# Clipped differences from stage one through DRAM, row statistics in the feed-forward, and cross attention in the order logits, values, transposes

## The chip, the cores and the metric

The kernel runs on one core of a Trainium2 chip. Its time is the device time of one execution in microseconds (us); lower is better. Before the change the median of three runs is 951.55 us (951.16 to 952.6). Five engines work side by side, each through its own list of instructions in program order: TensorE (PE; its weight loads are listed apart as PEld), VectorE (DVE), ScalarE (ACT), GpSimd (POOL) and SyncE (SP), which here issues all transfers. A "shape" such as 32*128 behind a matmul is the part of the TensorE array that it uses.

## What is computed

One decoder layer in float32, on 16 sequences of 256 tokens of width 256 (4096 rows). `n()` is a row norm without parameters; cut to what matters:

```python
# stage one: "attention" of 4 heads of 64 against 256 fixed keys and values
xn = n(x) * ln_g + ln_b
h  = n(2 * x + values(square(relu(scores(xn)))))
# cross attention: 16 heads of 16, keys and values from ctx of the same sequence
D    = clip(frac[:, None, :] - frac[:, :, None], -0.2, 0.2)
bias = alpha_pos * max(D, 0) + alpha_neg * min(D, 0)      # per head
attn = gamma * (Q K^T) / 4 + delta * bias
h    = n(h + softmax(attn) V Wo^T + bo)
# feed-forward: the arg-max gate of 8 chooses a rank-4 addition inside the relu
out  = n(h + relu(h Wi^T + bi + lora[top1]) Wo2^T + bo2)
```

The clipped differences, `min(D, 0)` and `max(D, 0)`, depend on `frac` alone. They are the same for all 16 heads of a sequence and need neither stage one nor the context.

## The kernel before

All work stands under a manual schedule: each engine executes its instructions in the order in which the Python code emits them, and only semaphores hold an engine back. So the order of the calls in the main loops is the order on every engine's list.

**Stage one** (about 12 to 258 us) takes 8 blocks of 512 tokens, each in 8 steps `m` of two pieces. A step's scores (L306), the relu on ACT (L314) and the square on DVE (L316) feed the next step's values matmuls (L326). What else belongs to a step (statistics, norms, turns of neighbouring blocks) is put into the list `steps[m]`, which is worked off after the step's matmuls. The result stays in SBUF as `hid`.

**Cross attention** (about 258 to 668 us) runs over 16 batches (the sequences) of 4 groups of 4 heads, in one loop over iterations `n`. The names of its parts, with their lines:

- `logits` (L583): 8 matmuls of shape 32*128 that add to four PSUM banks, `banks[0..3]`, in which `positive` (ACT, L574) has already put `alpha_pos * max(D, 0)`, one instruction for each of the four heads. A bank's `positive` for the next group can start only when its maxima are done.
- `negative` (L562 on POOL for three heads, L567 on ACT for the fourth) makes `alpha_neg * min(D, 0)`.
- `maxima` (DVE, L597): 8 instructions, each adds `neg` to half a bank, writes `t` to SBUF and gives the row maximum. `subtract` (L612) takes the maximum away, two heads on POOL and two on DVE.
- `turned(g)`: 4 transposes (PE, L621) of one head, and the exponential (ACT, L626) that brings them to `pT`.
- `attend` (PE, L635): 16 weight loads of shape 128*32; the weights are the probabilities' counterpart `va`, values with a column block of ones, so that the sums of the softmax come with the products. `keep` copies the two halves of a batch's result to `raw` (ACT, L648), and after the second half `gather` sends it through SP: sums (L493) and values `v` in 8 transfers (L501).
- `invert` (DVE L509; SP: rows L511, invs in 8 transfers L517) and `divide` (DVE L524) give the normalised heads; `project` (PE L531, DVE L540) adds the output projection to `hid`; `stats` makes the row statistics of the sum (L194 and L195, two rows of 128 tokens).
- For the next batch: `load` (context `cT` L392 and fractions `frow` L394), the hidden-state turn `turned` of the batch (4 transposes L403, ACT copy L410), `queries` (PE L416, ACT L426), `keys` (PE L436, DVE L446, then 8 transfers `kM` on SP, L452), `vals` (PE L458, DVE copy L466) and the two clips `below` and `above` (DVE L473).

PSUM has four logits banks, one for `attend`, and a ring of three banks from `tile_b()` that all else shares in turn: whoever gets a bank waits until the third allocation before it has been read.

An iteration emits, before the change: logits(n); transposes 2 and 3 of group n-1; negative(n+1); maxima(n); positive 0 and 1; subtract(n); positive 2 and 3; the large piece of this iteration; attend(n-1); transposes 0 and 1 of n; keep(n-1); further small work. The `pieces` function says which: a batch's first group has the hidden-state turn as small piece and `project` as large piece, the second `queries`, the third `keys`, the fourth `vals`; `invert` and `below` are at the second group, `above` at the third, `divide` at the fourth, `stats` at the first.

**The feed-forward** (about 668 to 948 us) takes 8 blocks of 512 tokens: `norm` (from the statistics in `mv2`), turn, gates, `inner`, `lora`, `outer`, and the final norm and store, each block's parts between those of its neighbours.

## Time and profile before

| | |
|---|---|
| median of 3 runs | 951.55 us (951.16 to 952.6) |
| the profiled execution | 950.16 us |
| its span, first to last instruction | 948.3 us (1.86 us lie around it) |
| granted TensorE clock | 0.99 |
| busy PE, DVE, ACT, POOL | 910.5, 692.3, 582.5, 427.4 us |
| period of a group of the cross attention | 5.90 to 5.92 us, at a batch's first group 6.38 us |
| a batch | 24.10 us undisturbed, 24.29 us on average over batches 2 to 13 |

How to read the profile: it is one execution, its times in us from the span's start. A line of the timeline gives start, length, engine, source line, operation, output<-inputs, shape and, after x, how many instructions in a row it stands for; in brackets is the idle time before it and who ended it. A line of the window view gives a stretch, its length, then busy time and number of instructions for PE, PEld, DVE, ACT and POOL, and last the granted clock, the share of the DMA engines and GB/s. "SPq" lines are issues of transfers on SP's queue. The chain of waits follows the work that ended last back to its start and shares out the span over engines.

### The profile page before, as it was taken

The numbers are of one execution on the slowest core, as the hardware profiler recorded it, in microseconds if no ns is written. First come the engines' busy times: TensorE is split into PE (matmuls) and PEld (weight loads), VectorE is DVE, ScalarE is ACT, GpSimd is POOL, SyncE is SP. The second block draws the span as 40 slices with busy tenths as digits, with TensorE's granted clock in tenths as the row PEclk, the third lists the DMA queues.
The fourth block names the chain that finished last, engine by engine and source line by source line (L and its number), as shares of the span: only waits on it lengthen the run. The fifth ranks groups of instructions, "written<-read, shape, count | busy, mean of one in ns | idle before, by whom it ended". The sixth has DMA issues, their size and how long they took to land.

```text
span 948.3 us, 19070 instructions
## 1 busy us (share of the span) xinstructions
PE 910.5 (96%) x6910; PEld 547.2 (58%) x6910; DVE 692.3 (73%) x1893; ACT 582.5 (61%) x970; POOL 427.4 (45%) x352
## 2 busy tenths in 40 slices
PE   5999999999988999999999999998789999999997
PEld 2333333333356677777777777775336566665656
DVE  4787879888777999999999999998523344343324
ACT  4757787677779899999999999997101010101010
POOL 1002321223467898999988889995101101110100
PEclk9999999999989999999999999999899999999999
DMA  5300000100101122222222222111100000000001
GB/s 156 116 23 23 8 17 23 40 2 2 28 1 40 46 51 52 54 53 53 53 53 53 53 51 54 47 43 25 24 1 0 23 23 2 21 23 23 1 22 45
DMA packets 42461, 33.85 MB, mean 36 GB/s; under 512 B 14720, under 2 KB 39808, under 8 KB 42368
## 3 DMA queue, kind: packets, MB, share of 16 engines
q1 hardware_dynamic: 41648, 31.85, 12.7%
q8 instruction: 55, 0.90, 0.4%
q10 hardware_dynamic: 720, 0.79, 0.4%
q14 instruction: 38, 0.31, 0.1%
HBM read 19.50 MB, written 4.46 MB: 25 GB/s over the span
## 4 chain that ended last, share of the span: by engine, by line
PE 88%; DVE 4%; ACT 3%; POOL 3%; issue 1%; DMA 1%; SPq 0%; POOLq 0%; ACTq 0%; DVEq 0%
PE ps_b L621 13%; PE ps_l L774 12%; PE ps_a L306 12%; PE ps_v L326 11%; PE ps_v L804 10%; PE ps_l L583 7%; PE ps_v L635 5%; PE ps_b L531 3%; PE ps_b L436 3%; POOL t L612 2%; PE ps_b L416 2%; PE ps_b L458 2%; PE ps_l L786 2%; DVE t L597 2%; PE ps_b L804 1%
## 5 line engine op out<-in xcount | busy, mean ns | idle before, releaser
L562 POOL TENSOR_SCALAR neg<-dneg,aneg,delta 128x512 f32<-128x512 f32 x192 | 228.0, 1198 | 0.0
L597 DVE CUSTOM_DVE_ANT_0 t<-ps_l,neg 128x256 f32<-128x256 f32 x512 | 181.5, 419 | 13.1 <-PE ps_l L583 6.6
L316 DVE TENSOR_TENSOR pr<-r 128x1024 f32<-128x1024 f32 x128 | 155.2, 1253 | 42.3 <-ACT r L314 42.1
L314 ACT ACTIVATE r<-ps_a 128x1024 f32<-128x1024 f32 x128 | 126.5, 1023 | 60.8 <-PE ps_a L306 36.4
L574 ACT ACTIVATE ps_l<-dpos,apos_d 128x512 f32<-128x512 f32 x256 | 162.8, 689 | 1.7 <-DVE mx L597 1.6
L626 ACT ACTIVATE pT<-ps_b 128x512 f32<-128x512 f32 x256 | 137.4, 594 | 32.8 <-PE ps_b L621 32.7
L621 PE MATMUL ps_b<-ident,t 128*128 128x128 f32 x1024 | 142.0, 282 | 11.7 <-POOL t L612 10.1
L621 PEld LDWEIGHTS ps_b<-ident,t 128*128 128x128 f32 x1024 | 110.9, 142 | 61.5 <-POOL t L612 33.5
L612 POOL TENSOR_TENSOR t<-t,mx 128x1024 f32<-128x1024 f32 x64 | 121.1, 1893 | 52.8 <-DVE mx L597 49.1
L306 PE MATMUL ps_a<-xnT,kT 64*64 64x512 f32 x1024 | 123.5, 597 | 0.2
L326 PE MATMUL ps_v<-pr,vv 64*64 64x512 f32 x1024 | 122.7, 592 | 0.0
L774 PE MATMUL ps_l<-xt,wi 128*128 128x512 f32 x256 | 114.4, 600 | 0.0
L704 POOL TENSOR_TENSOR x<-x,wofb 128x256 f32<-128x256 f32 x32 | 22.2, 730 | 202.7 <-PE ps_b L698 202.7
L793 ACT ACTIVATE hT<-ps_l,wib 128x512 f32<-128x512 f32 x32 | 20.3, 684 | 151.9 <-PE ps_l L786 137.4
L612 DVE TENSOR_TENSOR t<-t,mx 128x1024 f32<-128x1024 f32 x64 | 111.8, 1747 | 2.2
L804 PE MATMUL ps_v<-wof,hT 128*128 128x256 f32 x448 | 101.4, 382 | 0.0
L804 PEld LDWEIGHTS ps_v<-wof,hT 128*128 128x128 f32 x448 | 83.5, 190 | 18.9 <-issue 8.4
L338 POOL TENSOR_TENSOR xt<-xt,half 128x512 f32<-128x512 f32 x16 | 25.0, 1561 | 151.2 <-ACT half L337 151.2
L797 DVE TENSOR_SCALAR hT<-ps_l,wib 128x512 f32<-128x512 f32 x32 | 22.5, 746 | 88.7 <-PE ps_l L786 88.7
L774 PEld LDWEIGHTS ps_l<-xt,wi 128*128 128x128 f32 x256 | 48.4, 194 | 55.0 <-issue 55.0
L583 PE MATMUL ps_l<-kM,qT 32*128 32x256 f32 x1024 | 78.6, 405 | 0.0
L326 PEld LDWEIGHTS ps_v<-pr,vv 64*64 64x64 f32 x1024 | 38.6, 132 | 69.1 <-issue 42.3
(104 smaller groups left out, 1046.9 us busy)
## 6 DMA issues: line engine op xcount, KB each, us to landing
cT<-in_ctxT SPq DMA_DIRECT2D x16, 256.0 KB, 3.0
kM<-keys SPq DMA_DIRECT2D x128, 32.0 KB, 1.9
v<-raw SPq DMA_DIRECT2D x128, 32.0 KB, 2.0
invs<-rows SPq DMA_DIRECT2D x128, 32.0 KB, 1.8
x<-in_x SPq DMA_DIRECT2D x7, 512.0 KB, 4.1
out<-res SPq DMA_DIRECT2D x7, 512.0 KB, 2.9
frow<-in_frac SPq DMA_DIRECT2D x16, 128.0 KB, 3.4
wi<-in_wiT SPq DMA_DIRECT2D x1, 1024.0 KB
```

Source lines behind the costliest of these rows:

```text
L306: nc.tensor.matmul(sc[64 * k : 64 * k + 64, h, :], lhsT=kT[64 * h : 64 * h + 64, q, hf * P + 64 * k : hf * P + 64 * k + 64], rhs=self.xnT[ ...
L316: nc.vector.tensor_tensor(pr, r, r, ALU.mult)
L326: nc.tensor.matmul(self.acc[k][64 * h : 64 * h + 64, :], lhsT=vv[64 * k : 64 * k + 64, hf, 64 * q : 64 * q + 64], rhs=pr[64 * k : 64 * k + ...
L562: nc.gpsimd.tensor_scalar(self.neg[:, g], self.batch.dneg, aneg[:, h : h + 1], delta, ALU.mult, ALU.mult,)
L574: nc.scalar.activation(banks[g], self.batch.dpos.rearrange("p j k -> p (j k)"), AF.Copy, scale=apos_d[:, h : h + 1],)
L583: nc.tensor.matmul(banks[g][:, j * S : (j + 1) * S], lhsT=self.batch.qT[rows, self.o, j * P : (j + 1) * P], rhs=self.batch.kM[rows, self.i ...
L597: nc.vector.tensor_tensor_reduce(out=self.t[:, g, j, :], in0=banks[g][:, j * S : (j + 1) * S], in1=self.neg[:, g, j, :], scale=1.0, scalar ...
L612: eng.tensor_tensor(rows, rows, top.to_broadcast([P, 4, S]), ALU.subtract)
L621: nc.tensor.transpose(ps[:, k * S + j * P : k * S + (j + 1) * P], self.t[:, g, j, k * P : (k + 1) * P], ident,)
L626: nc.scalar.activation(self.pT[:, g, :], ps, AF.Exp)
L774: nc.tensor.matmul(banks[g], lhsT=wi[:, c, f * P : (f + 1) * P], rhs=self.xT[:, c, :], start=(c == 0), stop=False,)
L804: nc.tensor.matmul(ps[:, at * C : (at + 1) * C], lhsT=self.hT[f][:, j * P : (j + 1) * P], rhs=wof[:, f, :], start=(f == 0), stop=(f == FC ...
```

## The change

1. **Clips.** The two clips of batches 2 to 15 are made by DVE in stage one, in listed steps of blocks 1 to 7, and stored to DRAM (256 KB each); those of batches 0 and 1 are made there too and stay in SBUF. In the cross attention `reload` brings a batch's two clips back, two batches ahead, on SP. The fractions are loaded in stage one.
2. **Statistics.** `stats` is gone from the cross attention; `norm` of the feed-forward makes the four row statistics of its block.
3. **Order of an iteration.** Logits(n); attend(n-2); transposes 0 and 1 of n-1, whose exponentials stand between the positives on ACT (positive 0, 1, exp 0, positive 2, exp 1, positive 3); large piece; transposes 2 and 3 of n-1 with their exponentials; small piece. One iteration more is needed to drain.
4. **Pieces.** `queries` at a batch's first group (its ACT half after the last exponentials), `project` and gather at the second, `keys` and `invert` at the third, `vals`, the reload, and the hidden-state turn of the batch after next at the fourth; `divide` at the end of the next first group. The `raw` copy of a batch's first half moves from ACT to DVE.
5. **Seams.** The first feed-forward block's norm, turn and gates move into the last two iterations, and in the first block of the feed-forward the last batch's `divide` and `project`, `inner(1)` and `turn_um` change places with their neighbours.

```diff
...
-    mv2 = const.tile([P, NT, 2], FP, name="mv2")
...
                 nc.sync.dma_start(out=self.cT, in_=ctx_view[self.b])
-                self.frow = p2.tile([P, S], FP, tag="frow", name="frow")
...
+            def fractions(self):
+                self.frow = p2.tile([P, S], FP, tag="frow", bufs=3, name="frow")
...
+            def reload(self):
...
+                self.dneg = p2.tile([P, 2, S], FP, tag="dneg", name="dneg")
+                nc.sync.dma_start(out=self.dneg, in_=self.away["dneg"])
+                self.dpos = p2.tile([P, 2, S], FP, tag="dpos", name="dpos")
+                nc.sync.dma_start(out=self.dpos, in_=self.away["dpos"])
...
-            def below(self):
-                self.dneg = self.cut("dneg", 0.0, -CLAMP)
...
-            def above(self):
-                self.dpos = self.cut("dpos", CLAMP, 0.0)
+            def clip(self, name):
...
+                t = self.cut(name, *((0.0, -CLAMP) if name == "dneg" else (CLAMP, 0.0)))
+                if self.b < 2:
+                    setattr(self, name, t)
+                else:
+                    if not hasattr(self, "away"):
+                        self.away = {}
+                    self.away[name] = drams.tile(
+                        [P, 2, S], FP, tag=f"{name}{self.b}", bufs=1, name="away"
+                    )
+                    nc.sync.dma_start(out=self.away[name], in_=t)
...
-            def stats(self):
-                for j in range(2):
-                    row_stats(hid[:, 2 * self.b + j, :], mv2[:, 2 * self.b + j, :])
...
                     self.pT = pm.tile([P, 4, 2 * S], FP, tag="pT", name="pT")
-                ps = tile_b()
+                    self.ps = {}
+                ps = self.ps[g] = tile_b()
...
                         )
-                nc.scalar.activation(self.pT[:, g, :], ps, AF.Exp)
...
+            def exps(self, g):
+                nc.scalar.activation(self.pT[:, g, :], self.ps[g], AF.Exp)
...
                         batch.raw = pm.tile([P, 2, 512], FP, tag="raw", name="raw")
-                    nc.scalar.copy(batch.raw[:, self.o, :], batch.av)
-                    if self.o == 1:
+                    if self.o == 0:
+                        nc.vector.tensor_copy(batch.raw[:, self.o, :], batch.av)
+                    else:
+                        nc.scalar.copy(batch.raw[:, self.o, :], batch.av)
...
             b, og = divmod(n, 4)
-            nxt, last, older = (
-                batches[b + d] if 0 <= b + d < B else None for d in (1, -1, -2)
+            ahead, nxt, last, older = (
+                batches[b + d] if 0 <= b + d < B else None for d in (2, 1, -1, -2)
...
             if og == 0:
-                return (
-                    nxt and nxt.turned(), older and older.project(), [older and older.stats]
-                )
+                return nxt and nxt.queries(), None, [older and older.divide]
             if og == 1:
-                return None, nxt and nxt.queries(), [last and last.invert, nxt and nxt.below]
+                return older and older.project(), None, []
             if og == 2:
-                return None, nxt and nxt.keys(), [nxt and nxt.above]
-            return None, nxt and nxt.vals(), [last and last.divide]
+                return nxt and nxt.keys(), None, [last and last.invert]
+            return nxt and nxt.vals(), ahead and ahead.turned(), [ahead and ahead.load]
...
                 tb = self.tb
-                mv = mv2[:, 4 * tb : 4 * tb + 4, :]
+                mv = small.tile([P, 4, 2], FP, tag="mv", name="mv")
+                for j in range(4):
+                    row_stats(hid[:, 4 * tb + j, :], mv[:, j, :])
...
+        clips = [(batches[b], which) for b in [*range(2, B), 0, 1] for which in ("dneg", "dpos")]
+        slots = [(1, (5, 6, 7)), *((tb, (0, 3, 5, 6, 7)) for tb in range(2, 5))]
+        slots += [(5, (0, 5, 6, 7)), (6, (0, 5, 6, 7)), (NB - 1, (0, 1, 2, 3, 4, 5))]
+        slots = [(tb, m) for tb, ms in slots for m in ms]
+        assert len(slots) == len(clips)
...
                     steps[m].append(lambda: next(output))
+            for k, ((at, m), (batch, which)) in enumerate(zip(slots, clips)):
+                if at == tb:
+                    if k == 0:
+                        for ahead, _ in clips[0:4:2]:
+                            steps[1].append(ahead.fractions)
+                    if which == "dneg" and k + 4 < len(clips):
+                        steps[m].append(clips[k + 4][0].fractions)
+                    steps[m].append(lambda batch=batch, which=which: batch.clip(which))
...
                 steps[3].append(first.load)
+                steps[5].append(batches[1].load)
             if tb + 1 == NB:
-                steps[3] += [first.below, first.above]
...
-        for n in range(N + 1):
-            now, nxt, last = (
-                groups[n + d] if 0 <= n + d < N else None for d in (0, 1, -1)
+        for n in range(N + 2):
+            now, nxt, last, older = (
+                groups[n + d] if 0 <= n + d < N else None for d in (0, 1, -1, -2)
             )
-            small_piece, large_piece, more = pieces(n)
-            if n % 4 == 0 and n // 4 + 1 < B:
-                batches[n // 4 + 1].load()
+            large_piece, small_piece, more = pieces(n)
+            if n == 0:
+                small_piece = batches[1].turned()
+            if n % 4 == 3 and n // 4 + 2 < B:
+                batches[n // 4 + 2].reload()
...
                 step(early[3])
-            if last:
-                last.turned(2)
-                last.turned(3)
+            if older:
+                older.attend()
+            if n == 0:
+                step(small_piece)
+                step(small_piece)
...
                 now.maxima()
-            step(small_piece)
...
                 nxt.positive(1)
-            step(small_piece)
+            if last:
+                last.turned(0)
+                last.exps(0)
+            if nxt:
+                nxt.positive(2)
+            if last:
+                last.turned(1)
+                last.exps(1)
+            if nxt:
+                nxt.positive(3)
...
                 step(early[3])
-            if nxt:
-                nxt.positive(2)
-                nxt.positive(3)
+            if older and older.o == 1:
+                older.keep()
             step(large_piece)
-            step(large_piece)
-            if last:
-                last.attend()
+            if n % 4 > 0:
+                step(large_piece)
+            if older and older.o == 0:
+                older.keep()
...
                 rows_in[NB - 1].measure_out(n)
-            if now:
-                now.turned(0)
-                now.turned(1)
+            if n == N:
+                block.turn()
             if last:
-                last.keep()
+                for g in range(2, 4):
+                    last.turned(g)
+                    last.exps(g)
+            if n == N:
+                block.gates()
+            if n % 4 == 0:
+                step(large_piece)
+            step(small_piece)
+            step(small_piece)
...
                 rows_in[NB - 1].norm_out(by[NB], n - 4, n - 4, nc.vector)
+            if n == N - 1:
+                block = rows_out[0]
+                block.norm()
         end = batches[B - 1]
-        block = rows_out[0]
         add = end.project()
-        block.norm()
-        block.turn()
-        block.gates()
-        end.invert()
...
         block.inner(0)
+        end.invert()
         block.turn_um()
-        end.divide()
...
                     now.inner(0)
+                if tb == 1:
+                    now.turn_um()
...
             if tb == 0:
-                step(add)
-                step(add)
-                end.stats()
+                end.divide()
...
                 nxt.turn()
+            if now:
+                now.inner(1)
...
             if now:
-                now.inner(1)
...
                 nxt.gates()
+            if tb == 0:
+                step(add)
+                step(add)
...
                 last.store()
-            if nxt:
+            if nxt and last:
```

## The prediction

> **What bounds the kernel now.** I read the page's totals and its chain first, then the busy time of each engine in three stretches, then the timeline of one group of the cross attention. From the page:
>
> ```profile
> PE 910.5 (96%) x6910; PEld 547.2 (58%) x6910; DVE 692.3 (73%) x1893; ACT 582.5 (61%) x970; POOL 427.4 (45%) x352
> ...
> PE 88%; DVE 4%; ACT 3%; POOL 3%; issue 1%; DMA 1%; SPq 0%; POOLq 0%; ACTq 0%; DVEq 0%
> ```
>
> The chain lies on TensorE for 88% of the span. The windows (stretch, its length, then busy time of PE, weight loads, DVE, ACT, POOL) say how close the others follow:
>
> ```profile
> 12.00:258.00 246.00, 244.76 (x2174) 93.45 (x2176) 200.28 (x293) 176.70 (x234) 56.26 (x46) 1.00 0.10 30
> 258.00:668.00 410.00, 395.03 (x3656) 284.53 (x3648) 383.15 (x1289) 371.51 (x665) 345.07 (x254) 0.99 0.19 46
> 392.00:444.00 52.00, 52.00 (x501) 37.73 (x500) 51.00 (x169) 48.81 (x89) 47.56 (x35) 1.00 0.22 52
> ```
>
> Stage one is full on PE and leaves DVE 46 us. In the steady cross attention four engines are within 10% of full, so which of them ends a group has to be read from the timeline. The weight loads (PEld) of one group and of the start of the next, by start and length:
>
> ```profile
> 436.82 0.77 PEld L583 LDWEIGHTS ps_l<-kM,qT 32*128 32x128 f32 x16 [0.17 <-ACT ps_l L574]
> 437.92 0.85 PEld L621 LDWEIGHTS ps_b<-ident,t 128*128 128x128 f32 x8 [0.33 <-DVE keys L446]
> 438.75 1.60 PEld L458 LDWEIGHTS ps_b<-wv,cT 128*128 128x128 f32 x8
> 440.67 0.59 PEld L635 LDWEIGHTS ps_v<-pT,vaug 128*32 128x32 f32 x16 [0.33 <-ACT neg L567]
> 441.70 0.86 PEld L621 LDWEIGHTS ps_b<-ident,t 128*128 128x128 f32 x8 [0.44 <-POOL t L612]
> 442.73 0.77 PEld L583 LDWEIGHTS ps_l<-kM,qT 32*128 32x128 f32 x16 [0.17 <-ACT ps_l L574]
> 443.83 0.85 PEld L621 LDWEIGHTS ps_b<-ident,t 128*128 128x128 f32 x8 [0.33 <-issue]
> ```
>
> Logits to transposes 1.10, transposes to values projection 0.83, that to attend 1.92, attend to transposes 1.03, transposes to logits 1.03: 5.91 us with no long wait in it, so PE's own sequence is the bound. Eight transposes take 1.03 when another shape of the array follows (128*128 to 32*128) and 0.83 when the same shape does: a change of shape costs 0.20. The starts of the first maximum (S below) repeat that: 5.90 to 5.92 apart, and 6.38 at a batch's first group, which also holds the hidden-state turn and the output projection. A batch is 24.10 undisturbed, 24.29 on average over batches 2 to 13. DVE in the same group:
>
> ```profile
> 438.13 0.41 DVE L597 CUSTOM_DVE_ANT_0 t<-ps_l,neg 128x256 f32<-128x256 f32 x1
> ...
> 441.00 1.73 DVE L612 TENSOR_TENSOR t<-t,mx 128x1024 f32<-128x1024 f32 x1
> 442.65 0.68 DVE L466 COPY vaug<-ps_b 128x512 f32<-128x512 f32 x1
> 443.25 0.67 DVE L524 TENSOR_TENSOR oT<-v,invs 128x512 f32<-128x512 f32 x1
> 444.02 0.42 DVE L597 CUSTOM_DVE_ANT_0 t<-ps_l,neg 128x256 f32<-128x256 f32 x1
> ```
>
> S is 438.13, 1.31 after the logits' first load (1.29 for the next group). The subtraction starts at S+2.87, the values copy at S+4.52 and ends at S+5.20.
>
> **The new order of a group.** PE: logits(n), attend(n-2), transposes 0 and 1 (n-1), large piece, transposes 2 and 3. The array now changes shape three times a group instead of four, so PE alone would need 5.91 less 0.20, as at the transposes, or at most less 0.32, which is all that lies between the end of the projection's loads (438.75 + 1.60) and the attend's first: 5.59 to 5.71. Two waits stand in the way.
>
> The first is ACT's order: positive 0, 1, exp 0, positive 2, exp 1, positive 3. Transposes 3 get the PSUM bank of transposes 1 (a ring of three banks: t0, t1, large, t2, t3 puts t2 in t0's place and t3 in t1's), so they wait for exp 1. The first positive waits for two maxima, as here (its first maximum stands at 263.75):
>
> ```profile
> 264.63 0.69 ACT L574 ACTIVATE ps_l<-dpos,apos_d 128x512 f32<-128x512 f32 x1 [1.63 <-DVE mx L597]
> ```
>
> That is S+0.88. Then by the spacing of such instructions: positive 1 at 1.57, exp 0 at 2.18, positive 2 at 2.67, exp 1 at 3.28 to 3.87 (0.594 each on the page), load of transposes 3 at 3.92; half of a 1.03 slot and the shape change, 0.62, gives logits at S+4.54 and the next S at S+5.83. Bounds: 5.59 (the wait hidden) and 5.91. At the second group of a batch the query pair (1.01 on ACT) makes ACT late; I take 5.91 there.
>
> The second is at a batch's fourth group, where the hidden-state turn of batch b+2 now follows the values projection, transposes 2 and 3: the third bank after the values', so the same one. It waits for DVE's values copy, which program order puts behind eight maxima and the subtraction: S+5.20, load at 5.25. PE would be there at 4.34 (4.54 less the shape change). The turn and the shape change take 0.55, logits at S+5.81, next S at S+7.12. Bounds: 5.59+0.53 = 6.12 without the wait, 7.12 with it. The rows place the copy, so I take 7.12. The batch: 5.83 + 5.91 + 5.83 + 7.12 = 24.69, plus 0.59 on 24.10; the 0.19 of hiccups is taken as before. Twelve batches: +7.1. With the bounds: 22.9 (three of 5.59 and 6.12) to 24.9 (three of 5.91 and 7.12).
>
> The Trainium skill, Perfetto Trace Analysis, Matmuls, says that independent matmul groups should rotate through different PSUM banks so that evacuation overlaps the next group. Both orders rotate; by the rule alone the turn waits for nothing, the fourth group takes 6.12 and the batch 23.7, which would make the sum -7 instead of +5.4; the rows 442.65 and 0.68 say that a rotation of three is too short there.
>
> What is queued behind: DVE loses two clips (0.99 beside POOL and 0.67 here) and the statistics (1.18) and gains one raw copy (0.68) per batch; ACT loses one 0.59 copy. Neither is the bound. POOL keeps three negations (3 x 1.20) and one subtraction (1.89), 5.5 a group, just under 5.59. The Trainium skill, SBUF — State Buffer, Terms, calls the port pair of DVE and GpSimd an exclusive lock whose loser fully blocks; the clip's 0.69 alone and 0.99 beside POOL show 0.30 of it, not a whole negation of 1.20.
>
> **SP's queue.** Between raw copy and division it issues, in the new order, sums, v x8, kM x8, rows, invs x8, and the division stands on DVE ahead of the next second group's maxima. Such a run before:
>
> ```profile
> 427.16 5.12 SPq L501 DMA_DIRECT2D v<-raw  x8
> 432.38 0.53 SPq L511 DMA_DIRECT2D rows<-inv  x1
> 434.04 3.61 SPq L517 DMA_DIRECT2D invs<-rows  x8
> ```
>
> Sums 0.66, v 5.12, kM 8 x 0.632 = 5.06, rows 1.66 until invs, 3.61 and 1.8 to landing, division 0.68: 18.6 from the raw copy's end at S+5.1, so 23.7 of the 24.7. The slack is 1.0; single issues show hiccups of about 1 us. I price it at nothing; if each batch loses half a hiccup, +6. The two reloads and cT go behind invs and are needed over 15 us later (cT lands in 3.0).
>
> **Stage one.** Thirty more clips at 0.61 spacing (0.69 the row) are 18.3 to 20.7 us of DVE, between products:
>
> ```profile
> 242.60 0.69 DVE L473 CUSTOM_DVE_ANT_1 dneg<-frow,nfcol 128x512 f32<-128x512 f32 x1
> ```
>
> DVE has 46 us free, mostly at steps 0, 6 and 7 of a block (2.16, 1.44, 0.95 idle a step). Exposed: step 3 of three blocks and four steps of the last, 0.3 each: +2. Bounds: 0 and +20.7. Nothing leaves stage one but two clips, which are counted. Its stores (30 x 256 KB) run on a queue with 0.10 of the DMA time used.
>
> **The rest.** Batches 0 and 1 take 31.4 and 27.8 us before, with DVE behind; 3.4 us of clips leave them: -1.2 (a third), bounds -3.4 and +1. Batch 14 has no turn at its end: 23.4 for 24.1, -0.7. The last batch's three periods lose their projection slots: 16.4 for 18.2, -1.8. The drain has two iterations instead of one but takes the first feed-forward block's turn and gates in: 0, bounds -1.5 and +1.5. The row statistics become four pairs per block, 2.2 us of DVE, in a stretch where DVE is busy 105 of 280: 0 (they end at 6.7 after the LoRA step, the turn comes at 8.1); without that cover 8 x 2.2 = +17.5.
>
> **Sum:** 7.1 + 2 - 1.2 - 0.7 - 1.8 + 0 = +5.4. The profiled execution took 950.16 (span 948.3 and 1.86 around it), giving 955.6; the median of the runs stands 1.4 above it: 957.
>
> **Rivals.** (1) The order gains, on the other side: the values copy is done before PE reaches the turn. Its place is the fourth group, its price 1.0 a batch; it decides if the copy ends before S+4.34, 0.86 earlier than read. Against it: DVE's order. Then a batch is 23.7 to 23.9, where SP's chain (23.7) sets a floor: 12 x -0.3 and the rest's -1.7 give -5, 946; without the floor 22.9 gives -16, 935. 0.2. (2) The terms cancel: batch 24.25, 950 to 953.4, within 0.2% (1.9 us, about what measurement can tell from no change). 0.1. (3) SP's chain is late by half a hiccup a batch: 963. For it: the slack of 1.0; against it: v starts as soon as raw is done. 0.1. (4) Stage one's cover fails: all clips exposed, up to 976, more likely 965 to 972, since DVE idles only in parts of a block. 0.05. The forecast itself, 953.5 to 961: 0.55.
>
> **Chances and range.** Slower 0.55 + 0.1 + 0.05 = 0.7, same 0.1, faster 0.2. The range 944 to 966 leaves out the lower part of rival 1 and most of rival 4, under 0.2 in all; it takes in the half-hiccup and the rest's bounds.
>
> **What would show it.** Right: in the after-trace the fourth group's load of the hidden-state turn waits about 0.9 on DVE's values copy, periods near 5.83, 5.91, 5.83, 7.1, transposes 3 released by exp 1, stage one ending 2 us later. Wrong: fourth-group periods near 6.2, waits on DVE's division behind invs, products of stage one late by 0.6 a clip, or PE in the feed-forward waiting for statistics.

## The result, and the profile after

The changed kernel takes 967.75 us (median of 4 runs, 966.08 to 968.68) against 951.83 (951.16 to 952.6) of the kernel before: a ratio of 1.0165, 95% interval 1.0147 to 1.0183. It is slower, as forecast, but by 15.9 us instead of 5.4, and 1.75 us over the upper end of the range. Its profiled execution took 968.68 us (span 966.9), the slowest of its four; that of before, 950.16, lay under its median. So the traces differ by 18.6 us, 2.6 more than the medians, and the terms below add up to 18.6. For two of the kernels further down (the swap alone, and exponential 1 ahead of positive 2 without the spread pieces) the profiled execution ran at a granted clock of 0.56 and 0.85; their times are from other executions and their traces are not read.

The page of the changed kernel, busy time and then the chain's shares:

```profile
PE 911.5 (94%) x6910; PEld 545.7 (56%) x6910; DVE 708.4 (73%) x1909; ACT 585.3 (61%) x956; POOL 413.6 (43%) x352
...
PE 52%; DVE 8%; ACT 3%; issue 2%; SPq 1%; DMA 1%; ACTq 0%; DVEq 0%
```

PE has the same work (911.5 for 910.5) in 18.6 us more, and its share of the chain fell from 88% to 52%. The windows (stretch, length, then busy PE, PEld, DVE, ACT, POOL) show it in stage one and in ten batches or so of the cross attention, here of the changed kernel:

```profile
12.00:258.00 246.00, 240.56 (x2116) 88.39 (x2118) 222.16 (x319) 171.16 (x226) 50.98 (x41) 1.00 0.22 67
355.00:607.00 252.00, 242.79 (x2280) 178.28 (x2276) 220.66 (x750) 226.43 (x400) 208.19 (x160) 1.00 0.25 66
```

and here ten batches of the kernel before:

```profile
347.00:590.00 243.00, 242.82 (x2280) 178.09 (x2279) 237.03 (x800) 226.73 (x410) 218.34 (x161) 1.00 0.22 52
```

Before, PE is full; after, it does the same 2280 matmuls with the same 242.8 us and stands still for 9. The saved change of shape is not to be seen, because waits cost more than it gave. DVE is less busy (220.7 for 237.0) and nothing became shorter for it.

Where the 18.6 us of the span lie, by the start of each group's first maximum:

| part | predicted | measured |
|---|---|---|
| stage one (first maximum 270.94, before 263.75) | +2 | +7.2 |
| batches 0 and 1 (31.65 + 27.87, before 31.39 + 27.79) | -1.2 | +0.3 |
| batches 2 to 13 (302.4, before 291.5) | +7.1 | +10.8 |
| batch 14 (23.88 for 24.15) | -0.7 | -0.3 |
| batch 15, three periods (19.7 for 18.2) | -1.8 | +1.5 |
| from the last maximum to the end (290.5 for 291.5) | 0 | -1.0 |

An undisturbed batch has the periods 5.80, 5.91, 6.10 and 7.15, together 24.95; predicted were 5.83, 5.91, 5.83 and 7.12. The weight loads of the third and the fourth group of batch 4 in the changed kernel:

```profile
392.05 0.74 PEld L592 LDWEIGHTS ps_l<-kM,qT 32*128 32x128 f32 x16 [0.17 <-DVE t L621]
393.12 0.15 PEld L647 LDWEIGHTS ps_v<-pT,vaug 128*32 128x32 f32 x6 [0.33 <-ACT pT L638]
393.54 0.57 PEld L647 LDWEIGHTS ps_v<-pT,vaug 128*32 128x32 f32 x10 [0.26 <-ACT pT L638]
394.52 0.86 PEld L631 LDWEIGHTS ps_b<-ident,t 128*128 128x128 f32 x8 [0.41 <-POOL neg L571]
...
402.67 1.11 PEld L631 LDWEIGHTS ps_b<-ident,t 128*128 128x128 f32 x8
404.71 0.42 PEld L409 LDWEIGHTS ps_b<-ident,hid 128*128 128x128 f32 x4 [0.94 <-DVE vaug L472]
405.30 0.74 PEld L592 LDWEIGHTS ps_l<-kM,qT 32*128 32x128 f32 x16 [0.17 <-issue]
```

The turn at 404.71 waits 0.94 for the values copy, as predicted. At 393.54 the attend stops in the middle for an exponential, which was not predicted: from its start to the transposes is 1.40 there and 1.00 in the other groups. DVE beside it, and at the last batch:

```profile
402.32 1.74 DVE L621 TENSOR_TENSOR t<-t,mx 128x1024 f32<-128x1024 f32 x1
403.98 0.68 DVE L472 COPY vaug<-ps_b 128x512 f32<-128x512 f32 x1
...
664.25 0.69 DVE L537 TENSOR_TENSOR oT<-v,invs 128x512 f32<-128x512 f32 x1 [2.95 <-DMA invs<-rows]
```

S is 399.44: the copy starts at S+4.54 (predicted 4.52). At 664.25, in the last batch's first group, the division of batch 13 waits 2.95 for SP's chain, with the next maxima behind it; that first group lasts 8.17.

### The profile page after: what moved, and what is told of

It reads as the page before. It is cut to its first block, busy times and chain, and to the rows that moved or that the text cites. A ratio compares the mean times of both kernels' runs of the same rounds, so it can differ in the third digit from the quotient of the medians.

```text
span 966.9 us, 19117 instructions
## 1 busy us (share of the span) xinstructions
PE 911.5 (94%) x6910; PEld 545.7 (56%) x6910; DVE 708.4 (73%) x1909; ACT 585.3 (61%) x956; POOL 413.6 (43%) x352
## 4 chain that ended last, share of the span: by engine, by line
PE 52%; DVE 8%; ACT 3%; issue 2%; SPq 1%; DMA 1%; ACTq 0%; DVEq 0%
PE ps_l L788 12%; PE ps_v L818 10%; PE ps_b L631 7%; PE ps_l L592 6%; PE ps_v L647 4%; DVE t L606 3%; DVE t L621 2%; PE ps_b L442 2%; PE ps_b L544 2%; PE ps_l L800 2%; PE ps_b L422 2%; PE ps_b L818 1%; ACT ps_l L583 1%; ACT pT L638 1%; PE ps_b L712 1%
## 5 line engine op out<-in xcount | busy, mean ns | idle before, releaser
L571 POOL TENSOR_SCALAR neg<-dneg,aneg,delta 128x512 f32<-128x512 f32 x192 | 214.0, 1124 | 0.0
L583 ACT ACTIVATE ps_l<-dpos,apos_d 128x512 f32<-128x512 f32 x256 | 175.9, 693 | 36.4 <-DVE mx L606 23.6
L313 DVE TENSOR_TENSOR pr<-r 128x1024 f32<-128x1024 f32 x128 | 160.7, 1295 | 24.1 <-ACT r L311 23.8
L631 PE MATMUL ps_b<-ident,t 128*128 128x128 f32 x1024 | 144.4, 281 | 13.3 <-ACT pT L638 12.3
L638 ACT ACTIVATE pT<-ps_b 128x512 f32<-128x512 f32 x256 | 144.5, 595 | 3.5 <-PE ps_b L631 2.9
L631 PEld LDWEIGHTS ps_b<-ident,t 128*128 128x128 f32 x1024 | 113.5, 141 | 56.2 <-ACT pT L638 20.5
L335 POOL TENSOR_TENSOR xt<-xt,half 128x512 f32<-128x512 f32 x16 | 24.9, 1558 | 151.1 <-ACT half L334 151.1
```

The costliest lines, as they stand in the source:

```text
L313: nc.vector.tensor_tensor(pr, r, r, ALU.mult)
L571: nc.gpsimd.tensor_scalar(self.neg[:, g], self.batch.dneg, aneg[:, h : h + 1], delta, ALU.mult, ALU.mult,)
L583: nc.scalar.activation(banks[g], self.batch.dpos.rearrange("p j k -> p (j k)"), AF.Copy, scale=apos_d[:, h : h + 1],)
L631: nc.tensor.transpose(ps[:, k * S + j * P : k * S + (j + 1) * P], self.t[:, g, j, k * P : (k + 1) * P], ident,)
L638: nc.scalar.activation(self.pT[:, g, :], self.ps[g], AF.Exp)
```

## The experiments

Unless another base is named, an edit is made to the changed kernel. Ratios are to the kernel before, run on the same chip; its medians there were 949.6, 952.6, 951.2 and 951.1. Periods and starts are those of the profiled execution.

**Stage one: which clips cost.**

```diff
-        slots = [(1, (5, 6, 7)), *((tb, (0, 3, 5, 6, 7)) for tb in range(2, 5))]
+        slots = [(1, (5, 6, 7)), *((tb, (0, 5, 6, 7, 7)) for tb in range(2, 5))]
```

> The changed kernel with one edit: in blocks 2, 3 and 4 of stage one the clip of step 3 goes to step 7, beside the one there. Theory A (a clip at step 3 stands between the row statistics and the squares; the relu's second buffer then waits for a late square, and the values matmuls of the next step 1.0 us for that, 1.5 in all): step 5 of these blocks is 3.43 again instead of 4.9, the cross attention's first maximum comes 4.5 us earlier than at 270.9, total 963.3. Theory B (a clip costs DVE's stretch the same wherever it stands): the loss moves to another step, first maximum still near 270.9, total 967.8.

Measured: 964.7 us, ratio 1.0149 (1.0121 to 1.0177). The first maximum comes at 267.44, 3.5 earlier. Counted from one step's first score matmul to the next step's, the clip of step 3 is felt in step 5: that step of blocks 2 to 4 is 3.43 again (4.94, 4.90, 4.94 in the changed kernel). Step 3 of blocks 3 to 5, each behind a block that now has two clips at step 7, has grown from 3.97 to 4.23. Theory A holds for the 4.5; 0.8 of it comes back as a lag of DVE, which is what Theory B said of the whole. The changed kernel behind the clip of step 3 of block 2, on DVE:

```profile
93.74 0.69 DVE L479 CUSTOM_DVE_ANT_1 dneg<-frow,nfcol 128x512 f32<-128x512 f32 x1
94.35 3.44 DVE L313 TENSOR_TENSOR pr<-r 128x1024 f32<-128x1024 f32 x2
97.71 0.41 DVE L191 BATCH_NORM_STATS2 st<-x 128x6 f32<-128x256 f32 x1
```

and on PE:

```profile
95.72 1.09 PE L323 MATMUL ps_v<-pr,vv 64*64 64x512 f32 x8
97.84 1.09 PE L323 MATMUL ps_v<-pr,vv 64*64 64x512 f32 x8 [1.03 <-DVE pr L313]
```

One clip of 0.6 became a wait of 1.03 on PE, and 1.5 in the step: the two squares, 2.33 long together elsewhere, take 3.44, because the relu that the second needs had waited on ACT for a square:

```profile
95.66 1.02 ACT L311 ACTIVATE r<-ps_a 128x1024 f32<-128x1024 f32 x1 [0.53 <-DVE pr L313]
```

On PE the kernel without step 3 has this stretch without a gap:

```profile
95.76 1.90 PE L323 MATMUL ps_v<-pr,vv 64*64 64x512 f32 x16
```

**Stage one: the clips left out.** The reloads fetch batch 2's clips for all batches.

```diff
...
-        slots = [(tb, m) for tb, ms in slots for m in ms]
+        clips = clips[:2] + clips[-4:]
+        slots = [(1, 5), (1, 6), (7, 2), (7, 3), (7, 4), (7, 5)]
```

> The changed kernel without the clips of batches 3 to 15 in stage one and their stores; the reloads fetch batch 2's clips for every batch (so the biases of the other batches are not computed). Six clips stay. Theory A (the clips' time on DVE is the whole of stage one's loss): steps 3 and 5 of blocks 2 to 6 are as before the change, the first maximum comes at 264.5 to 265.5 instead of 270.9, total 961 to 962. Theory B (part of the loss comes from the loads of the fractions, the stores or the last block's order): the first maximum stays over 267. The periods of the cross attention stay as in the changed kernel in both.

Measured: 959.75 us, ratio 1.0071 (1.0051 to 1.0092); first maximum at 263.54. The steps of blocks 2 to 6 are as before the change to 0.01, only step 4 of the last block keeps 0.50. The 26 clips (with their stores and fractions, left out with them) are all of stage one's loss, and the undisturbed batches stay at 24.95. Theory A, with 1 to 2 us more gained than it said.

**The first part of the change alone** (clips, stores and reloads), in the kernel before:

```diff
...
-    return None, nxt and nxt.queries(), [last and last.invert, nxt and nxt.below]
+    return None, nxt and nxt.queries(), [last and last.invert]
-    return None, nxt and nxt.keys(), [nxt and nxt.above]
+    return None, nxt and nxt.keys(), []
...
+            if n % 4 == 3 and n // 4 + 2 < B:
+                batches[n // 4 + 2].reload()
```

> The kernel before with the first part of the change alone: the clips made in stage one at the same steps, stored and reloaded; the order of the cross attention, its pieces and the statistics as before. Theory A (the loop before is bound by PE's own sequence, so that clips taken from DVE bring nothing there): first maximum 7.2 later, batches 24.1 to 24.3 as before, total 957 to 959. Theory B (the clips were what disturbed batches, 24.29 against 24.10, and the first two): up to 4 come back, total 953 to 956.

Measured: 958.1 us, ratio 1.0083 (1.0062 to 1.0105). The first maximum comes 7.7 later; batches 0 and 1 take 31.40 and 27.82, as before the change; batches 2 to 13 take 24.21 on average (24.29 before). Theory A: in the old order the clips on DVE cost nearly nothing, and taken out of the loop they bring 1 us there and cost 7.7. So the predicted -1.2 for the first two batches was not the clips' to give.

**The copy first.**

```diff
-            if now:
+            if now and n % 4 < 3:
                 now.subtract()
...
+            if now and n % 4 == 3:
+                now.subtract()
```

> The changed kernel with one edit: in a batch's fourth group DVE's values copy stands ahead of the subtraction, so that the bank of the hidden-state turn is free at S+4.2 instead of S+5.2. Theory A (this wait alone sets the fourth group): its period falls from 7.15 to 6.2, a batch from 24.95 to 24.0, total 956.5. Theory B (behind it stands SP's chain from raw copy to division, 24.4 us long with the waits of this trace: the division of the undisturbed batches ends 0.5 before the maxima that follow it): the wait on the copy goes too, but the first group's period grows from 5.80 to 6.2, the batch is 24.4 and every hiccup of SP counts in full: total 961 to 965.

Measured: 966.3 us, ratio 1.0163 (1.0131 to 1.0196). The wait is gone: the fourth group lasts 6.27. But the first groups now last 6.46 to 6.54 in seven batches, 7.2 to 7.8 in four and 8.06 in the last (5.80 in most, before the edit). DVE in that kernel, fourth group of batch 4 and then the next first group:

```profile
402.84 0.69 DVE L472 COPY vaug<-ps_b 128x512 f32<-128x512 f32 x1 [0.80 <-PE ps_b L464]
403.45 1.27 DVE L621 TENSOR_TENSOR t<-t,mx 128x1024 f32<-128x1024 f32 x1
...
411.06 0.95 DVE L537 TENSOR_TENSOR oT<-v,invs 128x512 f32<-128x512 f32 x1 [0.98 <-DMA invs<-rows]
```

Theory B in its mechanism, with a total 1.3 over what it said: behind the copy stood SP's chain. Over the cross attention DVE waits 20.0 us for invs instead of 9.1. The usual batch went from 24.95 to 24.61 and batches 2 to 13 together from 302.4 to 298.8; batches 1 and 14, 1.8 longer than in the changed kernel, took back half of that.

**The division a group later**, keys and projection swapped:

```diff
             if og == 0:
-                return nxt and nxt.queries(), None, [older and older.divide]
+                return nxt and nxt.queries(), None, []
             if og == 1:
-                return older and older.project(), None, []
+                return nxt and nxt.keys(), None, [older and older.divide]
             if og == 2:
-                return nxt and nxt.keys(), None, [last and last.invert]
+                return older and older.project(), None, [last and last.invert]
```

> The changed kernel with one edit: keys and projection change places (second and third group) and the division goes from the end of the first group to the end of the second, one group (5.9 us) later against SP's chain. Theory A (in batches 3, 7, 9, 13, 14 and 15 the late division lengthens the first group: 1.41, 0.85, 0.67, 0.09, 0.17 and 2.37 over 5.80, together 5.6): first groups are 5.80 in all batches, total 962.3. Theory B (the division now makes DVE's list in the second group 2.87 + 1.65 + 0.80 + 0.68 = 6.0 long, over the period of 5.90): the second group's period grows by 0.1 to 0.5 in every batch and takes most of it back, total 965 to 968.

Measured: 966.7 us (966.6 to 970.9), ratio 1.0185 (1.0146 to 1.0224): no gain that can be told from none, and the total of Theory B, without a trace that says why. (The projection of the last batch but one stands behind the loop here.)

> Both edits of the two runs before together. If the copy's wait and SP's chain are the two bounds of a batch, one behind the other, the gain of both is more than the sum of the single ones: batch 24.0, first groups 5.80, fourth 6.2, total 951. If the wait alone bounds it: 956.5 or less the 5.6 of the late divisions, 951 as well, but then the run with the copy alone shows 956.5. If DVE's list in the second group is the next bound: 953 to 956.

Measured: 967.3 us (963.5 to 969.8; the profiled execution is the fastest), ratio 1.0173 (1.0132 to 1.0215), against all three expectations. First groups are 5.80 to 5.83 and fourth ones 6.27, as expected; second groups are 5.96, but 9.69, 8.02, 7.54, 7.65 in batches 3, 5, 7 and 9 and 6.3 to 6.8 in batches 11 to 14. SP's queue of that kernel, and its loads:

```profile
360.42 0.36 SPq L400 DMA_DIRECT2D dneg<-away  x1
360.88 0.38 SPq L402 DMA_DIRECT2D dpos<-away  x1
361.34 0.38 SPq L389 DMA_DIRECT2D cT<-in_ctxT  x1
```

```profile
361.71 0.86 PEld L631 LDWEIGHTS ps_b<-ident,t 128*128 128x128 f32 x8 [0.41 <-issue]
364.84 2.96 PEld L442 LDWEIGHTS ps_b<-cT,wk 128*128 128x128 f32 x8 [2.27 <-issue]
```

The keys, one group earlier, wait for the context, whose issue stands behind invs and the two reloads: 361.34 and 3.0 to landing is 364.3. The next run tests that reading.

**The context earlier**, on top of both:

```diff
-                return nxt and nxt.queries(), None, []
+                return nxt and nxt.queries(), None, [ahead and ahead.load]
...
-            return nxt and nxt.vals(), ahead and ahead.turned(), [ahead and ahead.load]
+            return nxt and nxt.vals(), ahead and ahead.turned(), []
```

> The last kernel with both edits (copy first, keys and projection swapped) and one more: the context of the batch after next is loaded at the end of a batch's first group instead of the fourth, where its issue stands behind the eight invs and the two reloads. Theory A (with the keys a group earlier, the keys' matmuls waited for this load: second groups of 6.3 to 9.7 in batches 3, 5, 7, 9, 11 to 14): second groups are 5.96 in all batches, every batch 24.07, total 10 less than that kernel's 967, 957. Theory B (the second group waits for the division or its transfers): second groups over 6.3 stay, total over 963.

Measured: 952.5 us (10 runs), ratio 1.0000 (0.9987 to 1.0013). Batches 2 to 13 but one take 24.05 to 24.08, with 5.82, 5.96, 6.02 and 6.27. Theory A, and 4.5 us better than it said; it had taken 10 from the median of 967, while 10.7 lie between the two profiled executions. Three edits that each move one place in a queue take 15 us from the changed kernel, although the first two, alone or together, took 1 or none.

**Exponential 1 first**, on top of that:

```diff
+            if last:
+                last.turned(1)
+                last.exps(1)
             if nxt:
                 nxt.positive(2)
-            if last:
-                last.turned(1)
-                last.exps(1)
```

> As the kernel with the early context load, and one edit more: on ACT exponential 1 stands ahead of positive 2 instead of behind it, so that the bank for transposes 3 is free 0.6 earlier. Theory A (of the prediction: transposes 3 wait for exponential 1, and PE alone would need 5.59 to 5.71): first group 5.60 to 5.71 instead of 5.82, the batch 23.2 to 23.5, total 7 to 11 less than with the early load alone. Theory B (DVE's list of 6.0 in the second group, POOL's 5.5 and ACT's own list hold the period, not the bank): first group 5.8, less than 3 us gained.

Measured: 951.5 us, ratio 1.0000 (0.9986 to 1.0013). Theory B in its total. Transposes 3 did wait 0.20 for exponential 1 in a second group of the kernel that this one is built on (load at 435.76); what took the place of that wait, this run does not show.

**Lists of DVE and ACT spread** (on the copy first and the early context): the query pair on DVE, and

```text
first group:  queries; invert (older); load
second group: keys
third group:  vals; divide (older)
fourth group: project (older); turn of the batch after next
```

> The order of the change with copy first and the early context load, and the large pieces once more in another order: queries, keys, values, projection; the query pair goes from ACT to DVE, the reciprocal to the next batch's first group, the division to its third. DVE's list is then at most 5.7 us in a group and ACT's at most 5.5. Theory A (the second group's 5.96 comes from the query pair on ACT and from DVE's list of 6.0): second and third group near 5.8, batch 23.6 to 23.7 against 24.07, total 946 to 948. Theory B (the groups are bound by PE with the wait for exponential 1 and the lists are not the point): batch 24.0, total 951 to 953.

Measured: 953.4 us, ratio 1.0028 (1.0013 to 1.0043). The second group fell to 5.80 as Theory A says, the third is 6.10 (6.02 with the early context), batches are 23.9 to 24.3 and the total is 0.4 over Theory B's.

> As the run with the spread pieces, and exponential 1 ahead of positive 2. The same edit brought under 1 us where ACT and DVE had the longer lists. Theory A (with the lists shorter, the bank of transposes 3 is the bound): 5.80 to 5.65 in three groups, batch 23.1 to 23.3, total 940 to 943. Theory B (some other wait takes its place at once, as before): within 1.5 us of the run with the spread pieces alone.

Measured: 952.4 us, ratio 1.0013 (0.9999 to 1.0026): 5.83, 5.70, 6.19 and 6.27. Theory B again; what the second group gave the third took.

> As the run before it, with no clip at step 3 of blocks 2 to 4 (block 1: steps 3, 5, 6, 7; blocks 2 and 3: steps 0, 5, 6, 7 and a second one at 7; blocks 4 to 6: 0, 5, 6, 7). Expected from the run without step 3: the three losses of 1.5 at step 5 gone, 0.2 to 0.3 more at step 3 of two blocks: first maximum at 267 to 267.5 instead of 270.9, total 3.5 less than the run before it. If the early clip at block 1 waits for its fractions, block 1 is longer by 1 to 3.

Measured: 948.7 us, ratio 0.9970 (0.9955 to 0.9986). The first maximum comes at 266.5 instead of 270.7, and the total is 3.7 less: as expected. This one beats the kernel before, by 0.3%.

**The third group.**

```diff
-            if older and older.o == 1:
-                older.keep()
             step(large_piece)
...
                     last.exps(g)
+            if older and older.o == 1:
+                older.keep()
```

> The changed kernel with one edit: in a batch's second group ACT's copy of the second raw half stands behind exponentials 2 and 3 instead of ahead of them. In the changed kernel the attend of the third group waits 0.26 for exponential 3, and the third group's period is 6.10 where 5.83 was predicted. Theory A (that raw copy is why the exponential is late): the wait goes, the third group falls to 5.83, 12 to 14 times 0.27 = 3.5; the raw copy is 1.0 later, so SP's chain gives up to 0.5 a batch back at the first group. Theory B (attend then waits for its own PSUM bank, which the raw copy empties, as long as before): third group still 6.1.

Measured: 976.4 us, ratio 1.0246 (1.0225 to 1.0266). The third group stays at 6.10, Theory B: its attend now waits 0.73 for the raw copy itself (load at 394.68 in batch 4). The chain, which begins 1 us later, makes the first group 6.47 in seven batches, 7.2 to 7.7 in four and 8.60 in the last: some 8 us lost for one copy that comes 1 us later. The next run takes the copy off ACT.

```diff
-                        nc.scalar.copy(batch.raw[:, self.o, :], batch.av)
+                        nc.vector.tensor_copy(batch.raw[:, self.o, :], batch.av)
...
+            if older and older.o == 1:
+                older.keep()
             if now:
                 now.subtract()
```

> The changed kernel with one edit: in a batch's second group the copy of the second raw half goes from ACT to DVE, ahead of the subtraction, so at S+2.9 instead of S+5.1. Theory A (on ACT it stands between the positives and exponentials 2 and 3, which the attend of the third group waits for; behind them it kept the attend's bank instead; and SP's chain starts with it): third group 5.8 instead of 6.10, and the divisions come 1.6 earlier, so first groups are 5.8 in nearly all batches: batches of 24.65, 12 x 0.3 and up to 5.6 less, total 959 to 961. Theory B (the third group is held by something else, the chain by the eight values transfers wherever they start): third group 6.1, total over 965.

Measured: 963.9 us, ratio 1.0126 (1.0102 to 1.015). The third group is 5.80 in every batch, an undisturbed batch 24.66: Theory A there. Its loads show the attend in one piece, in the slot that took 1.40 in the changed kernel:

```profile
393.66 0.59 PEld L647 LDWEIGHTS ps_v<-pT,vaug 128*32 128x32 f32 x16 [0.33 <-issue]
394.66 0.86 PEld L631 LDWEIGHTS ps_b<-ident,t 128*128 128x128 f32 x8 [0.41 <-issue]
```

The late divisions stay (6.47 in batches 3, 6, 7, 9 and 14, 7.51 in the last), so for them Theory A falls, and the total lies between the two theories. SP's queue says why:

```profile
392.10 5.12 SPq L514 DMA_DIRECT2D v<-raw  x8
399.34 5.72 SPq L458 DMA_DIRECT2D kM<-keys  x8
```

The values are issued by 397.2, but kM waits for the keys until 399.3, and rows and invs wait in line behind kM. The chain has two beginnings, the raw copy and the keys.

**All together**: spread pieces, exponential 1 first, the other steps of stage one, and both raw copies on DVE ahead of the subtraction.

> The kernel with spread pieces, exponential 1 first and the other steps of stage one, and both raw copies on DVE ahead of the subtraction. Expected: the third group 6.19 falls to 5.70 to 5.85, the first 5.83 to 5.70 (its attend waited 0.13 for the first raw half), the batch from 24.0 to 23.4, the lower end that PE's own sequence of 5.70 and the turn's 0.59 leave; total 948.7 less 7, 942. If DVE's list in the second group (2.87 + 0.60 + 1.65 + 0.80 = 5.92) holds it, the batch is 23.6 to 23.7 and the total 944 to 945.

Measured: 942.7 us (6 runs, 941.29 to 945.77), ratio 0.9908 (0.9885 to 0.9932), 25 us under the changed kernel and 8.4 under the kernel before. Groups take 5.71, 5.77, 5.74 and 6.30, a batch 23.52. Its window over 11 batches, and its loads over one group:

```profile
349.00:608.00 259.00, 259.00 (x2500) 197.86 (x2496) 242.55 (x858) 232.87 (x407) 229.20 (x177) 1.00 0.27 70
```

```profile
382.72 0.74 PEld L592 LDWEIGHTS ps_l<-kM,qT 32*128 32x128 f32 x16 [0.17 <-issue]
383.80 0.59 PEld L647 LDWEIGHTS ps_v<-pT,vaug 128*32 128x32 f32 x16 [0.33 <-DVE keys L452]
384.80 0.86 PEld L631 LDWEIGHTS ps_b<-ident,t 128*128 128x128 f32 x8 [0.41 <-issue]
385.62 1.60 PEld L464 LDWEIGHTS ps_b<-wv,cT 128*128 128x128 f32 x8
387.25 1.01 PEld L631 LDWEIGHTS ps_b<-ident,t 128*128 128x128 f32 x8
388.43 0.81 PEld L592 LDWEIGHTS ps_l<-kM,qT 32*128 32x128 f32 x16 [0.17 <-issue]
```

PE is full again, DVE waits for invs nowhere in the loop, and the order's own price can be read: 1.08 + 1.00 + 0.82 + 1.63 + 1.18 = 5.71, against 5.91 before. The saved change of shape is worth 0.20 a group: the projection slot lost 0.29 (1.63 for 1.92), and the transposes ahead of the logits took 0.15 of that back (1.18 for 1.03).

## Why the prediction was wrong

**Right.** The slower sign; the wait of the hidden-state turn on the values copy, in its place, its cause and its size (copy at S+4.54 for 4.52, period 7.15 for 7.12); the wait for exponential 1 (in batch 5's first group transposes 3 load at S+3.92, as worked out, after a wait of 0.11; the group is 5.80 for 5.83); the second group (5.91 for 5.91); that PE alone needs 5.59 to 5.71 (5.71 in the last kernel). The Trainium skill (Perfetto Trace Analysis, Matmuls) has independent matmul groups rotate through different PSUM banks, so that the evacuation of one overlaps the next group's matmuls. In this case's rotation of three the turn waited in 12 of 12 batches, 8.4 us in all, by the waits of PE from 330 to 633 us in the changed kernel:

```profile
PE ps_b L409 <- DVE vaug L472: 8.4, 12, 0.7
PE ps_b L631 <- ACT pT L638: 2.2, 5, 0.6
```

**Wrong, in four terms.** The span went 18.6 up where 5.4 was summed; the 13.2 between them are:

- *Stage one, "exposed: step 3 of three blocks and four steps of the last, 0.3 each: +2"*: 7.2. The place (step 3 of three blocks) was right, and the largest part, 4.5, came from there. The size was wrong by five: 1.5 for a clip that was priced at 0.3. A delay on DVE was taken for a delay on PE of the part that doesn't fit into the gap. But square, relu and score go round through two relu buffers, so the late first square makes the relu late and the second square later still. The last block, at 0.9 in its step 3 and 0.5 in its step 4, is near the 1.2 summed for it. The remainder, 1.5, lies at step 3 of blocks 2 to 6 (0.1 to 0.4 each): a lag that DVE carries over from steps 5, 6, 7 and 0, where idle time had been counted as cover. It is gone without the clips and grows with a second one at step 7. (The first block gave 0.2 back.)
- *"5.83 + 5.91 + 5.83 + 7.12"*: the third group is 6.10. The raw copy on ACT, at its new place in the second group, puts exponentials 2 and 3 back, and the attend, which now comes right after the next logits, waits for the third of them. The text on ACT said that it loses a copy and is not the bound; it looked at how much is in the list and not at what stands ahead of what. 12 times 0.26 is 3.1.
- *"I price it at nothing" (SP's chain)*: in the loop its length and its slack were right. From the issue of `sums` to the end of the division a chain without hiccups takes 18.9, by the usual lengths of its parts in the changed kernel (0.66 for sums, v 5.12, 0.49 for the keys, kM 4.99, 1.72 for rows, invs 3.59, 1.6 to the division, 0.68 for it). In batch 4 the maxima behind the division come 19.86 after that issue: a slack of 1.0. (The 0.5 that the run with the copy first named is read from the end of that batch's division, which stands straight behind DVE's subtraction, and kM took 5.49 there.) In batches 2 to 13 the late divisions and hiccups cost 3.0, only 0.7 more than the 2.3 by which the batches of before lay over 24.10, which the sum had left in. The price fell at the end, where the sum made batches 14 and 15 shorter by 0.7 and 1.8. Without a turn the fourth group of batch 14 is 1.1 shorter (6.03 for 7.15), and that takes the whole slack; so the 2.3 of hiccups in its chain counted in full (v 6.28 for 5.12, 0.33 more ahead of it, 2.8 for 1.6 from the last issue to the division, less 0.4 at the keys):

```profile
643.76 0.62 SPq L506 DMA_DIRECT2D sums<-raw  x1
644.75 6.28 SPq L514 DMA_DIRECT2D v<-raw  x8
...
657.89 3.59 SPq L530 DMA_DIRECT2D invs<-rows  x8
```

  The last first group took 8.17, 2.4 over 5.80, and 7.5 to 8.6 in the five other traces with this order of pieces. With the loop's 0.7, and 1.3 by which these two batches' own periods were taken too short (6.10 and 6.03 in the third and fourth group, 5.8 for 5.5 in the last batch), that is 4.4. The rival named the mechanism for the loop, and the forecast forgot it where its own batches became shorter.
- *"-1.2 (a third)" for batches 0 and 1*: +0.3. A third of the clips' time had no row behind it, and the first part alone shows that these batches don't feel the clips.

The drain and the feed-forward gave 1.0 where 0 was taken. The row statistics, also priced at 0, do show at the seam: PE's turn of the second block waits 4.74 for the norm, and 2.2 of that are DVE's four pairs of statistics (702.26 to 704.48). From the third block on PE waits for none of them.

```profile
702.26 0.42 DVE L191 BATCH_NORM_STATS2 st<-hid 128x6 f32<-128x256 f32 x1
705.62 2.21 PE L712 MATMUL ps_b<-ident,x 128*128 128x128 f32 x8 [4.74 <-DVE x L203]
```

The range ended at 966 because the terms' upper bounds were given too little. Stage one's reached +20.7, and all that lay over +2 got a chance of 0.05; the batch's ended at 24.9, under the 24.95 that undisturbed ones took.

## What to carry to other kernels

Work moved off an engine that is not the bound brings next to nothing where it was (1 us here), and its price where it goes is not its length less the idle time there: look for a ring of buffers that the engine stands in, because one late link can cost a multiple of its own delay (1.5 us for 0.6 here). When an order is changed, follow for every engine what stands ahead of each instruction that another engine waits for, not how full the list is; and where one wait is taken away, ask at once what the next one is, since single edits to the changed kernel brought 4 us at most, one cost 8, and all of them together brought 25. A chain of small transfers through one queue is a floor under the period; how much slack it keeps must be asked for in every stretch that is to become shorter, the last one too.

## What was not expected of the hardware

Issues on SP of eight transfers, 5.0 to 5.1 us as a rule, took 5.5 to 6.3 in other batches (v at 342.00 and 368.25 in the changed kernel: 6.31 and 5.89). What makes a single issue longer was not found. They were there before the change too (v 6.27, 5.97 and 6.43 in batches 1, 7 and 8), often at the same batches, and cost more as soon as a division waited behind them.

Nine divisions on DVE in the changed kernel took 0.77 to 1.20 instead of 0.68. Each ended 0.54 to 0.55 after a POOL instruction that was running when it began: the one at 386.29 took 1.15, and POOL's negation ended at 386.90. The prediction's clips beside POOL had shown 0.30; in these nine the price was the rest of the POOL instruction, 0.1 to 0.5.

Eight transposes behind a projection of the same shape, ahead of logits of another shape, took 1.18 to the logits' first load, without a wait in the profile, where eight behind an attend took 1.03. It reads as part of a saved change of shape that comes back at the next one; no run tests that.
